# Scatters that add, and 13 of 16 feature groups held at once, in a segment-attention kernel

## Chip, cores and metric

The kernel runs on one core of one Trainium2 chip. The metric is the device time of one execution in microseconds (us), the median of several executions. Two sorts of chips took part. On those of the first sort the kernel before took 408 to 411 us (the first comparison and two of the four calls of experiments); on the quicker sort, 367 us (the other two calls). So times of different calls are not compared; ratios within a call, and lengths of stages within a trace, are. In the views of the profile PE is TensorE's matmuls, PEld its loads of weights, DVE VectorE, ACT ScalarE, POOL GpSimd and SPq the queue of SyncE; "issue" marks time in which an engine waited for nothing that the profile shows, "remote" a wait for something that it can't name.

## The reference

```python
# feat 16384 x 256 float32, bids: the segment (0..7) of each row, in no order
q, k, v = feat @ Wq, feat @ Wk, feat @ Wv          # dqk = 32
qp, kp, vp = pad(q), pad(k), pad(v)                # by segment, in order of rows, at most 3072
attn = softmax(where(mask, qp @ kp.T, NEG))        # pos = row number minus the first place of its segment
r = (attn @ vp)[bids, pos]
t = r @ Wt
tn = (t - t.mean(0)) / sqrt(t.var(0) + 1e-5) * gamma + beta
return feat + relu(tn)
```

The positions are computed as if the segments were sorted, and they are not, so most rows share one result. The kernel uses that: most rows of the output are `feat` plus one of a few rows `y`, and some 5,500 rows, the owners, have a result of their own.

## The kernel before

Attention goes segment by segment. GpSimd gathers the features of the owners into `xs` (48 tiles of 128 rows) and `xL` (3 tiles more, of rows found late). After the batch statistics the output stage has two parts. The dense part takes all 16384 rows as 16 groups of 1 MB: it loads a group, adds `hot.T @ y` to it and stores it. The owners' part normalises each owner's row, adds its features, and overwrites its row in the output by a scatter, after the dense store that it must follow. Overwriting needs the features of the owners in `xs` until the end.

```python
# attention, fifth segment: flags of edges, which the dense part needs as 0/1 matrices "hot"
for c in range(C):                                   # C = 8
    eb = hotp.tile([P, GT * P], BF16, tag="eb", bufs=2)
    nc.vector.memset(eb, 99.0)
    for r in range(2):
        nc.sync.dma_start(eb[64 * r : 64 * r + 3 * NE, :], edge_of[...].to_broadcast(...))
    nc.vector.tensor_scalar(hot[:, c, :, :], eb..., emod, None, ALU.is_equal)
# ... cut ...
# owners' rows, two tiles at a time: three VectorE passes, one of them with the features x
nc.vector.tensor_tensor(p, t, scale.to_broadcast([P, T, D]), ALU.mult)
nc.vector.tensor_tensor(p, p, shift.to_broadcast([P, T, D]), ALU.add)
nc.vector.scalar_tensor_tensor(t, p, 0.0, x, ALU.max, ALU.add)
# ... cut ...
for n, pair in enumerate(pairs):                     # 8 pairs of groups
    for k in pair:
        if k >= len(ahead):
            nc.sync.dma_start(f_bufs[k % IOB], feat3[ORDER[k]])     # IOB = 6 buffers
    for i in range(0, GT, 2):
        # ... TensorE: pf = hot.T @ y; in pairs 2 to 7 one of two groups also adds its features there ...
        # ... VectorE adds pf to the other group, ScalarE copies the first one back ...
        for _ in range(n_ops[n]):
            next(row, None)                          # a pass of the owners' rows
    for k in pair:
        dense.append(nc.scalar.dma_start(out3[ORDER[k]], f_bufs[k % IOB]).ins)
# ... cut ...
def put(y, at, after):                               # GpSimd, 48 + 3 times
    w = nc.gpsimd.indirect_dma_start(out=out, out_offset=..., in_=y, ...).ins
    for d in dense[after:]:
        tc.declare_no_dep(w, d)                      # waits for the first `after` stores only
```

Of the kernel before, what the change touches and what calls it, by code (L numbers as in the profile page):

```python
# [18 lines left out]
P = 128  # L19
# [16 lines left out]
IOB = 6  # L36
# [495 lines left out]
def segment_attention_bn_kernel(  # L532
# [44 lines left out]
    with ExitStack() as short:  # L577
# [49 lines left out]
        xL = fs.tile([P, LT, D], F32, name="xL")  # L627
# [35 lines left out]
        ]  # L663

# [207 lines left out]
        def list_tokens(e, h, pc):  # L872


            at = e * FT + 3 * h
            own3 = slice(at, at + 3)

            def col(c):
                return pc[:, :, c : c + 1].rearrange("p t x -> p (t x)")

            lr = fw.tile([P, 3], F32, tag="lr", name=f"lr_{e}")
            nc.vector.tensor_tensor(lr, rcol[:, 3 * h : 3 * h + 3], col(J), ALU.subtract)
            nc.vector.tensor_tensor(lr, lr, col(J + 1), ALU.subtract)
            jc = fw.tile([P, 3], F32, tag="jc", name=f"jc_{e}")
            for t in range(3):
                upto = fw.tile([P, J], F32, tag="upto", name=f"upto_{e}")
                nc.vector.tensor_scalar(
                    upto, pc[:, t, 0:J], lr[:, t : t + 1], None, ALU.is_le, ALU.add,
                    accum_out=jc[:, t : t + 1],
                )  # L890
            pad = fw.tile([P, 3], F32, tag="pad", name=f"pad_{e}")
            nc.vector.tensor_scalar(
                pad, valid[:, own3], 1.0, -float(N), ALU.subtract, ALU.mult
            )
            nc.vector.tensor_add(jc, jc, pad)
            nc.vector.tensor_tensor(idx[:, own3], jc, col(J + 2), ALU.add)
            for t in range(3):
                x = xs[:, at + t, :] if e < NB else xL[:, 3 * h + t, :]
                gather(x, feat, idx[:, at + t : at + t + 1], N)
# [164 lines left out]
        def attend(b, T):  # L1064
# [15 lines left out]
            if b == NB - 1:  # L1080
                nc.vector.tensor_add(E[:, 0, :], E[:, 0, :], e_late)
                nc.vector.tensor_mul(E[:, 1, :], E[:, 0, :], E[:, 0, :])
                for g, f in zip(ORDER, f_bufs):
                    nc.sync.dma_start(f, feat3[g])
                statistics()
# [280 lines left out]
        for a in range(NB // PART):  # L1366
# [4 lines left out]
            for arm in tc.Switch(tiles[a], 3**PART, hint=f"part{a}"):  # L1371

                T = [TMIN + arm // 3**i % 3 for i in range(PART)] + [FT]
                for i in range(PART):
# [11 lines left out]
                    if b + 1 < NB:  # L1386
                        first_scores(b + 1)
                    if b == 0:
                        positions()
                        load_reads(0)  # L1390
                        for x in (acc, E, xL, L, xs[:, (NB - 1) * FT :, :]):
                            zero(x.rearrange("p t d -> p (t d)"))
# [50 lines left out]
        def rows():  # L1443


            work = [(tk[:, ts(u, 2), :], xs[:, ts(u, 2), :]) for u in range(TT // 2)]
            for at in range(0, LT, 2):
                t = slice(at, min(at + 2, LT))
                work.append((L[:, t, :], xL[:, t, :]))
            for t, x in work:  # L1450
# [6 lines left out]
                yield  # L1457
                nc.vector.scalar_tensor_tensor(t, p, 0.0, x, ALU.max, ALU.add)  # L1458
# [9 lines left out]
        n_ops = [0, 0, 4, 4, 3, 3, 3, 3]  # L1468
        with tc.manual_schedule(engines={mybir.EngineType.DVE, mybir.EngineType.PE}):
            for n, pair in enumerate(pairs):  # L1470
                for k in pair:
                    if k >= len(ahead):
                        nc.sync.dma_start(f_bufs[k % IOB], feat3[ORDER[k]])
                for i in range(0, GT, 2):
# [3 lines left out]
                    for u in range(2):  # L1478
                        for k in pair:
                            half, c = ORDER[k] % 2, ORDER[k] // 2  # L1480
                            r = slice(64 * half, 64 * half + 3 * NE)
                            on_pe = n > 1 and k % 2
# [9 lines left out]
                    for k in pair:  # L1492
                        two = f_bufs[k % IOB][:, i : i + 2, :]
                        if n > 1 and k % 2:
# [5 lines left out]
                for k in pair:  # L1500
                    dense.append(nc.scalar.dma_start(out3[ORDER[k]], f_bufs[k % IOB]).ins)
                if n == 1:
# [12 lines left out]
        def put(y, at, after):  # L1515
# [6 lines left out]
                oob_is_err=False,  # L1522
            ).ins
# [61 lines left out]
```

## Time and profile before

| kernel before | value |
|---|---|
| runs ahead of the prediction | 409.6 us median of 3 (406.14 to 420.6) |
| the profiled execution | 397.4 us, span 395.6 us |
| statistics ready (first matmul that uses `y`) | 275.4 us |
| last matmul, after the statistics | +99.9 us |
| last scatter ends, after the statistics | +103.8 us |
| output stage: busy PE / DVE / ACT | 80.1 / 76.0 / 13.4 us of 99.9 |

The lines of the page and of the trace are shown in the prediction below. One reading of this table matters later: the profiled execution was 9 to 23 us quicker than the three timed ones.

### The profile page before, as it was taken

The page shows a single profiled execution, that of the slowest core. Times are in us where ns is not written, and L with a number is a line of the kernel's source. Part 1 is how long each engine was busy: PE and PEld are TensorE (multiplying, and loading weights), DVE is VectorE, ACT ScalarE, POOL GpSimd, SP SyncE. Part 2 cuts the span into 40 slices and gives each one's busy share as a digit, 9 for nine tenths or more (in the row PEclk, how much of TensorE's full clock was granted, in tenths as well). Part 3 has the DMA queues.
Part 4 walks back from the last instruction along what each step waited for, and adds up shares of the span by engine and source line. Part 5 has one row for each costly group of instructions (what it writes and reads, how often), then busy time and mean ns, then how long its engine had stood idle before and what let it go on. Part 6 is the DMA issues. An engine that isn't in the chain of part 4 may idle for free.

```text
span 395.6 us, 4145 instructions
## 1 busy us (share of the span) xinstructions
PE 288.5 (73%) x1139; PEld 178.3 (45%) x1139; DVE 262.8 (66%) x776; ACT 109.4 (28%) x208; POOL 170.2 (43%) x181
## 2 busy tenths in 40 slices
PE   1659596905889999389989499992897699099900
PEld 0436474603557578157855386661233243033300
DVE  8974699573778646488982166577999784198600
ACT  8424533202423541234233214530021110021100
POOL 3425166787540320377877400010314377454720
PEclk9978699977899999869999989996555555555555
DMA  5101012021121211211331010469799999745460
GB/s 109 35 14 56 5 56 86 11 74 50 43 59 58 65 35 55 60 44 40 100 107 49 0 51 30 160 231 368 284 398 370 397 400 381 275 178 235 177 240 4
DMA packets 20905, 53.34 MB, mean 135 GB/s; under 512 B 6606, under 2 KB 13344, under 8 KB 16746
## 3 DMA queue, kind: packets, MB, share of 16 engines
q1 hardware_dynamic: 11493, 25.06, 18.4%
q10 hardware_dynamic: 2421, 16.83, 10.4%
q0 software_dynamic: 6928, 10.81, 9.0%
q14 instruction: 48, 0.39, 0.4%
q8 instruction: 15, 0.25, 0.3%
HBM read 26.67 MB, written 29.92 MB: 143 GB/s over the span
## 4 chain that ended last, share of the span: by engine, by line
PE 46%; DVE 24%; issue 12%; another core or an unknown queue 5%; DMA 3%; ACT 3%; POOL 2%; DVEq 0%; POOLq 0%; ACTq 0%
PE po L1008 18%; PE pf L1488 8%; PE pv L953 7%; PE s L967 4%; DVE work L1497 3%; DMA work<-in_r_feat 3%; PE pf L1483 3%; PE px L922 2%; PE pqk L934 2%; POOL out L1516 2%; DVE tk L1013 2%; DVE py L1456 1%; DVE work L941 1%; DVE py L1454 1%
## 5 line engine op out<-in xcount | busy, mean ns | idle before, releaser
L1008 PE MATMUL po<-work 128*128 128x257 f32 x394 | 101.4, 405 | 14.0 <-issue 6.7
L1008 PEld LDWEIGHTS po<-work 128*128 128x128 f32 x394 | 77.4, 203 | 31.4 <-issue 10.3
L836 POOL DMA_INDIRECT xs<-in_r_feat,idx x48 | 50.9, 1061 | 64.8 <-issue 40.0
L1516 POOL DMA_INDIRECT out<-tk,idx x48 | 47.3, 984 | 45.0 <-DVE tk L1458 16.6
L836 POOL DMA_INDIRECT reads_r<-reads_of,idx x48 | 54.2, 1130 | 19.4 <-issue 15.1
L953 PE MATMUL pv<-wvt,work 128*128 128x256 f32 x164 | 39.4, 391 | 13.0 <-issue 11.6
L1483 PE MATMUL pf<-y,hot 48*128 48x256 bf16 x128 | 27.3, 391 | 20.4 <-ACT f L1495 9.5
L1488 PE MATMUL pf<-work,ident 128*128 128x256 f32 x64 | 39.0, 714 | 2.5 <-DMA work<-in_r_feat 2.5
L1497 DVE TENSOR_TENSOR work<-work,pf 128x512 f32<-128x512 f32 x40 | 26.1, 683 | 21.8 <-remote 14.4
L953 PEld LDWEIGHTS pv<-wvt,work 128*128 128x128 f32 x164 | 30.9, 193 | 21.3 <-issue 13.5
L972 ACT ACTIVATE work<-s,mask 128x512 f32<-128x512 f32 (+2 forms) x62 | 32.6, 601 | 17.7 <-PE s L967 12.4
L1012 DVE RECIPROCAL rdens<-po 128x1 f32<-128x1 f32 x39 | 6.1, 161 | 45.7 <-PE po L1008 21.4
L997 ACT ACTIVATE sq<-tk 128x256 f32<-128x256 f32 x39 | 16.3, 418 | 55.0 <-DVE tk L1013 47.4
L1483 PEld LDWEIGHTS <-hot 48*128 48x128 bf16 x128 | 7.1, 104 | 44.6 <-issue 44.5
L967 PE MATMUL s<-work 32*128 32x512 f32 (+2 forms) x124 | 24.8, 595 | 3.0 <-ACT work L972 3.0
L957 ACT COPY work<-pv 128x512 f32<-128x512 f32 (+1 forms) x21 | 12.1, 577 | 43.1 <-PE pv L953 25.3
L1495 ACT COPY work<-pf 128x512 f32<-128x512 f32 x16 | 9.4, 586 | 48.8 <-PE pf L1488 39.9
L922 PE MATMUL px<-ident,xs 128*128 128x128 f32 x82 | 15.8, 296 | 8.9 <-issue 2.9
L1488 PEld LDWEIGHTS pf<-work,ident 128*128 128x128 f32 x64 | 16.0, 310 | 11.8 <-issue 9.1
L934 PE MATMUL pqk<-work,wqk 128*128 128x512 f32 (+2 forms) x52 | 20.9, 539 | 0.2 <-issue 0.2
L998 DVE SCALAR_TENSOR_TENSOR acc<-sq,reads_r,acc 128x256 f32<-128x256 f32 x39 | 18.7, 481 | 1.2 <-ACT sq L997 0.7
L1488 PE MATMUL pf<-f,ident 128*128 128x256 f32 x32 | 19.5, 714 | 0.0
(241 smaller groups left out, 371.2 us busy)
## 6 DMA issues: line engine op xcount, KB each, us to landing
work<-in_r_feat SPq DMA_DIRECT2D x14, 1024.0 KB
out<-work ACTq DMA_DIRECT2D x14, 1024.0 KB
t_rows<-tk SPq DMA_DIRECT2D x3, 768.0 KB
t_rows<-tk SPq DMA_DIRECT2D x4, 512.0 KB
f<-in_r_feat SPq DMA_DIRECT2D x2, 1024.0 KB
out<-f ACTq DMA_DIRECT2D x2, 1024.0 KB
eb<-edge_of SPq DMA_DIRECT2D x16, 96.0 KB
t_rows<-tk SPq DMA_DIRECT2D x4, 256.0 KB
```

The lines of the kernel that those rows point to most:

```text
L836: nc.gpsimd.indirect_dma_start(out=dst, out_offset=None, in_=table, in_offset=bass.IndirectOffsetOnAxis(ap=ind, axis=0), bounds_check=n - ...
L922: nc.tensor.transpose(px[:, ts(t, P)], xs[:, b * FT + t0 + t, ts(h, P)], ident)
L934: nc.tensor.matmul(pqk[:, 0:w], wqk[:, h, :], xT[:, h, own_c], start=(h == 0), stop=(h == DH - 1),)
L953: nc.tensor.matmul(pv[:, t, :], xT[:, h, ts(t0 + t, P)], wvt[:, h, :], start=(h == 0), stop=(h == DH - 1),)
L967: nc.tensor.matmul(s[:, i, 0:w], k[g, t // 4, :], q[g, c : c + w], start=True, stop=True)
L972: nc.scalar.activation((pr_b if c else pr_a)[:, t, 0:w], s[:, i, 0:w], AF.Exp, bias=mask[:, m : m + 1],)
L998: nc.vector.scalar_tensor_tensor(acc[:, 1, :], sq, reads_r[:, one], acc[:, 1, :], ALU.mult, ALU.add)
L1008: nc.tensor.matmul(po, pr[:, t, ts(r, P)], v[:, t, :], start=(t == 0), stop=(t == T - 1))
L1483: nc.tensor.matmul(pfs[k][:, u, :], hot[r, c, i + u, :], y3[r, :], start=True, stop=not on_pe,)
L1488: nc.tensor.matmul(pfs[k][:, u, :], ident, f_bufs[k % IOB][:, i + u, :], start=False, stop=True,)
L1497: nc.vector.tensor_add(two, two, pfs[k])
L1516: w = nc.gpsimd.indirect_dma_start(out=out, out_offset=bass.IndirectOffsetOnAxis(ap=idx[:, at : at + 1], axis=0), in_=y, in_offset=None, b ...
```

## The change

The intent was to free the space of the owners' features. If the scatter adds to the output instead of overwriting it, the features are already there, put down by the dense store. `xs` is then dead after the projection, and six groups can be loaded onto it while attention still runs. One VectorE pass of the owners' rows goes away, and their ReLU moves to ScalarE. ScalarE gets more to do, so its stores go to SyncE.

```diff
-IOB = 6
+IOB = 13
-        xL = fs.tile([P, LT, D], F32, name="xL")
+        x_bufs = [xs[:, ts(g, GT), :] for g in range(TT // GT)]
+        f_bufs = x_bufs + f_bufs
@@ the loop over segments
                     attend(b, T[i])
                     if b + 1 < NB:
                         first_scores(b + 1)
+                    if b >= PART:                                  # PART = 4
+                        done = (b + 2) * FT
+                        for k in range(len(x_bufs)):
+                            if (done - FT if b > PART else 0) < (k + 1) * GT <= done:
+                                nc.sync.dma_start(x_bufs[k], feat3[ORDER[k]])
@@ owners' rows
-                nc.vector.scalar_tensor_tensor(t, p, 0.0, x, ALU.max, ALU.add)
+                nc.scalar.activation(t, p, AF.Relu)
@@ output stage
-        n_ops = [0, 0, 4, 4, 3, 3, 3, 3]
+        n_ops = [0, 2, 2, 2, 2, 2, 2, 2]
-                            on_pe = n > 1 and k % 2
+                            on_pe = n > 0 and k % 2
-                    dense.append(nc.scalar.dma_start(out3[ORDER[k]], f_bufs[k % IOB]).ins)
+                    dense.append(nc.sync.dma_start(out3[ORDER[k]], f_bufs[k % IOB]).ins)
+                    if k - 3 + IOB in range(IOB, NG):
+                        nc.sync.dma_start(f_bufs[k - 3], feat3[ORDER[k - 3 + IOB]])
@@ put
                 oob_is_err=False,
+                compute_op=ALU.add,
```

(Cut: the gathers and the zeroing of `xL`, the five loads onto `work`, and some reordering, among it that ScalarE's instructions of the output stage are put in a fixed order too.)

More of the change, by code (lines that the diff above doesn't have):

```diff
@@ L897, in list_tokens @@
             for t in range(3):
-                x = xs[:, at + t, :] if e < NB else xL[:, 3 * h + t, :]
-                gather(x, feat, idx[:, at + t : at + t + 1], N)
+                if e < NB:
+                    gather(xs[:, at + t, :], feat, idx[:, at + t : at + t + 1], N)
         def load_list(e):
@@ L1082, in attend @@
                 nc.vector.tensor_mul(E[:, 1, :], E[:, 0, :], E[:, 0, :])
-                for g, f in zip(ORDER, f_bufs):
-                    nc.sync.dma_start(f, feat3[g])
+                for k in range(len(x_bufs), len(f_bufs)):
+                    nc.sync.dma_start(f_bufs[k], feat3[ORDER[k]])
                 statistics()
@@ L1390, in segment_attention_bn_kernel @@
                         load_reads(0)
-                        for x in (acc, E, xL, L, xs[:, (NB - 1) * FT :, :]):
+                        for x in (acc, E, L, xs[:, (NB - 1) * FT :, :]):
                             zero(x.rearrange("p t d -> p (t d)"))
@@ L1443, in rows @@
         def rows():
-            work = [(tk[:, ts(u, 2), :], xs[:, ts(u, 2), :]) for u in range(TT // 2)]
-            for at in range(0, LT, 2):
-                t = slice(at, min(at + 2, LT))
-                work.append((L[:, t, :], xL[:, t, :]))
-            for t, x in work:
+            work = [tk[:, ts(u, 2), :] for u in range(TT // 2)]
+            work += [L[:, at : min(at + 2, LT), :] for at in range(0, LT, 2)]
+            for t in work:
                 T = t.shape[1]
@@ L1456, in rows @@
                 nc.vector.tensor_tensor(p, p, shift.to_broadcast([P, T, D]), ALU.add)
-                yield
-                nc.vector.scalar_tensor_tensor(t, p, 0.0, x, ALU.max, ALU.add)
+                nc.scalar.activation(t, p, AF.Relu)
                 yield
@@ L1467, in segment_attention_bn_kernel @@
         pairs = [(k, k + 1) for k in range(0, NG, 2)]
-        n_ops = [0, 0, 4, 4, 3, 3, 3, 3]
-        with tc.manual_schedule(engines={mybir.EngineType.DVE, mybir.EngineType.PE}):
+        n_ops = [0, 2, 2, 2, 2, 2, 2, 2]
+        for k in range(len(ahead), IOB):
+            nc.sync.dma_start(f_bufs[k], feat3[ORDER[k]])
+        with tc.manual_schedule(engines=set(ENGINES[:3])):
             for n, pair in enumerate(pairs):
-                for k in pair:
-                    if k >= len(ahead):
-                        nc.sync.dma_start(f_bufs[k % IOB], feat3[ORDER[k]])
                 for i in range(0, GT, 2):
@@ L1493, in segment_attention_bn_kernel @@
                         two = f_bufs[k % IOB][:, i : i + 2, :]
-                        if n > 1 and k % 2:
+                        if n > 0 and k % 2:
                             nc.scalar.copy(two, pfs[k])
@@ L1500, in segment_attention_bn_kernel @@
                 for k in pair:
-                    dense.append(nc.scalar.dma_start(out3[ORDER[k]], f_bufs[k % IOB]).ins)
-                if n == 1:
+                    dense.append(nc.sync.dma_start(out3[ORDER[k]], f_bufs[k % IOB]).ins)
+                    if k - 3 + IOB in range(IOB, NG):
+                        nc.sync.dma_start(f_bufs[k - 3], feat3[ORDER[k - 3 + IOB]])
+                if n == 0:
                     nc.vector.tensor_copy(scale[:, 0, :], scale_s)
```

## The prediction

> **What bounds the kernel now.** I read the page's picture of the span in 40 slices first, since the change touches one stage only, then the table of stretches, then the timeline of the last stage. A slice is 9.9 us.
>
> ```profile
> PE   1659596905889999389989499992897699099900
> DVE  8974699573778646488982166577999784198600
> PEclk9978699977899999869999989996555555555555
> DMA  5101012021121211211331010469799999745460
> ```
>
> The reader is to see three ages. Up to slice 26 (about 266 us) there is attention, with TensorE near full in most slices, near full clock, and little DMA. Then come the batch statistics, with TensorE idle. From 275 us on there is the output stage: clock 0.5, DMA at 9 for five slices and then at 4 to 7. In slices 34 and 35 PE falls to 0 and DVE to 1: something stops both.
>
> The table of stretches (engine busy us, then clock, DMA share, GB/s) cuts the last stage up:
>
> ```profile
> core 0: us, PE busy (x) PEld busy (x) DVE busy (x) ACT busy (x) POOL busy (x), PEclk, DMA share, GB/s
> ...
> 285.80:298.80 13.00, 10.51 (x31) 4.29 (x29) 12.66 (x22) 2.35 (x4) 2.10 (x3) 0.50 1.00 393
> ...
> 314.00:336.00 22.00, 21.27 (x58) 9.07 (x59) 13.11 (x21) 2.39 (x5) 16.82 (x18) 0.50 1.01 389
> 336.00:345.00 9.00, 0.37 (x1) 0.10 (x1) 0.00 (x0) 0.54 (x1) 5.09 (x6) 0.50 0.80 309
> ```
>
> From 286 to 336 the DMA engines are full at 390 GB/s; from 314 TensorE is full too; from 336 to 345 nothing computes. The timeline names the waits, and shows the step in which TensorE works and how the scatters are issued at the end:
>
> ```profile
> 298.75 1.22 PE L1488 MATMUL pf<-work,ident 128*128 128x256 f32 x2 [2.49 <-DMA work<-in_r_feat]
> ...
> 332.38 0.40 PE L1483 MATMUL pf<-y,hot 48*128 48x256 bf16 x2
> 332.71 0.50 PEld L1488 LDWEIGHTS pf<-f,ident 128*128 128x128 f32 x2 [0.22 <-issue]
> 332.71 1.22 PE L1488 MATMUL pf<-f,ident 128*128 128x256 f32 x2
> ...
> 345.06 0.69 DVE L1497 TENSOR_TENSOR work<-work,pf 128x512 f32<-128x512 f32 x1 [11.41 <-remote]
> ...
> 376.89 0.98 POOL L1516 DMA_INDIRECT out<-L,idx  x1 [0.30 <-issue]
> ...
> 378.18 0.99 POOL L1516 DMA_INDIRECT out<-L,idx  x1 [0.30 <-issue]
> ```
>
> So the output stage waits for feature groups: six buffers hold 16 groups, and a buffer is reloaded only after its store, behind a full DMA system. Between these waits TensorE sets the pace: the same 1.22 us piece begins every 1.48 us (332.71, 331.23, 329.75 in the timeline). The stage from 275.5 us to the last matmul at 375.3 us is 99.8 us: 9.6 us for the first two pairs, 48 steps (6 pairs of 8) x 1.48 = 71.0 us, and so 19 us of waits. The last scatter is issued at 378.2 us, the last stores at 377.7 to 378.5, and the span ends at 395.6: 17 us of landing and closing that no part of the change touches.
>
> **What the Trainium skill says.** "DMA: Bandwidth & Descriptors", section "SWDGE vs HWDGE vs iDMA", says that an accumulating DMA can be issued from GpSimd only; the scatters are already there, so no issue moves. It doesn't price an accumulate. "Collectives: The Full Stack", section "The bandwidth ceiling: the fold count and why AG ≠ RS ≠ AR", says that an add in flight reads two sources with two read descriptors, and so ran at half the rate of a copy. The trace of before has no accumulate, so it neither agrees nor differs. "DMA: Bandwidth & Descriptors", section "Issuing engines are not separate DMA queues", says that all issuers share the same 16 engines; the full DMA row with three queues active agrees. "TensorE: Matmul & The Clock Gate", section "Part 1: The HAM clock gate (the "warmup" mystery)", says that about 3.4 us of sustained work releases the full clock. The trace differs: from 314 to 336 us TensorE is 97% busy and its clock stays at 0.50. I go by the trace and keep 1.48 us a step.
>
> **The change part by part.**
> (a) Loads. Six groups go onto the space of `xs` after the fifth, sixth and seventh segments, five more onto `work` as before, two onto new tiles. So 13 of 16 are there or on the way as the stage begins, and the last three refill buffers whose stores finish two pairs into it. The 19 us of waits should vanish. The early loads (6 x 1.05 MB, 2.7 us each at 390 GB/s) fall between about 205 and 255 us, where the slices show under 110 GB/s and mostly far less.
> (b) VectorE. A pair of owners' tiles cost three passes of 0.69 us and now two; the third, a ReLU, goes to ScalarE. There are 24 whole items and 2 of `L`: 26 x 0.69 = 17.5 us leave VectorE. The adds of groups fall from 40 to 36, another 2.7. VectorE goes from the 76 us busy of 275.4 to 380 to about 56: per half-step 0.68 + 2 x 0.69 = 2.06 us against 2.96 us of TensorE. Not a bound.
> (c) TensorE. Pair 1 moves there as well, so 56 steps instead of 48: 56 x 1.48 = 82.9 us, 11.9 more, for one pair (about 4.8 us) less on VectorE. Stage: 4.8 + 82.9 = 87.7 us, from 275.5 to 363.2 instead of 375.3. Gain **12 us**: the waits of 19 us minus 7.
> (d) ScalarE. 28 copies instead of 24 and 26 ReLUs at about 0.59 us: 32 us, far from full. Its stores go to SyncE, which waits in order but carries few.
> (e) Scatters. The 51 are issued every 0.98 + 0.30 = 1.29 us. With an add, each of their some 5,500 rows of 1 KB also reads its old value: 5.6 to 6.5 MB more DMA reading, about the 6 MB of loads that leave the stage. The bytes of the stage stay near 33 to 35 MB, 85 to 90 us at 390 GB/s.
> When do they end? They wait for the first 3, 5, 7 or 11 stores, and for their rows, now one item per 2.96 us from 280: the last rows of the last segment at 351, of `L` at 357. Segments one to four need store 5, landed near 309, and then 24 scatters; in order, at 1.29 us, the last of 51 leaves at about 367, instead of 378.2. Gain **11 us**. I choose 10 as the sum of (c) and (e), which run side by side, less a microsecond for contention: span about 385.5, or 2.5% off.
> The clock of runs is not the profile: unprofiled runs gave 406 to 421, the profiled one 397. 409.6 x 0.975 is 399; I shade it to 398, since the stage suffers from full DMA and probably suffers more in the longer runs.
>
> **Rivals.**
> 1. The adding scatter becomes the bound. If three descriptors in place of two make its issue 1.9 us instead of 1.29, the last 45 after 309 us take 86 us and end at 395: slower than before by 17, near 425. At 1.6 us they end at 381 and nothing is gained. For it: two reads per row. Against it: gathers and scatters of different row sizes (4 bytes, 1 KB) all take 0.98 to 1.13 us here, so issue hardly depends on what is moved. Chance about 2 in 10 of losing most of the gain here.
> 2. The waits move into attention. Early loads share the DMA engines with gathers of indices' rows, and all engines but GpSimd stand still between 222 and 226 us for the last of such gathers. If 4 MB delay it, or block SyncE's row stores, 2 to 10 us come back. Against it: gathers have their own queue, and the DMA share there is 0.02. I count 1 us as likely: about 400.
> 3. The loads were hidden anyway and TensorE at half clock absorbs everything: pair 1 costs 12 us more on it. If only the 9 us standstill goes, gain is about 2, near 407.
> 4. TensorE, no longer starved, gets its full clock. Then DMA (88 us from 281, so 369) bounds, and no more than the 10 us come out. So the upside is short, except where the longer unprofiled runs gain more.
>
> **Range and chances.** 398 us as the middle; rivals 2 and 3 fill 400 to 412, a gain of 6% fills the other side: 384 to 412. Faster by over 2% means under 401.4: 0.57. Within 2%: 0.33. Slower needs rival 1 in full: 0.10.
>
> **What would show it.** In the trace of after: no waits for in_r_feat in the output stage and no standstill; TensorE steps still of 1.48 us and the last matmul near 363; scatters still about 1.29 us apart with the last near 367; ReLUs on ScalarE near 0.6 us; y ready near 275 as before. Scatters further apart than 1.5 us, statistics later than 278, or a clock other than 0.5 in the stage would each prove the sum wrong.

## The result

The changed kernel is correct and took **436.04 us** (434.32 to 436.54, 4 runs); the kernel before took 407.89 us (406.14 to 420.6, 4 runs). The ratio is **1.070**, 95% interval 1.064 to 1.077: slower. Ratios here and below are the mean time of one kernel's fast runs over the mean of the other's fast runs of the same rounds, so they are not quite the ratio of the medians.

The page's picture of the changed kernel, 40 slices of 10.8 us:

```profile
PE   1777696521999998475688999995699999994000
DVE  8972898206799737432369436467976756661000
POOL 3415247773050500377500550000107788888880
PEclk9989699955899999588689589999555555555555
DMA  4101012100222102481014301377999989999530
```

In the output stage PE is 9 from slice 29 to 35, without the fall to 0 that the picture of before has in slice 34 (the prediction says 34 and 35, but 35 is a 9 again): the standstill is gone, and TensorE waits for no load, as predicted. But a new row is full: POOL is at 8 for the last seven slices with work, two of them wholly after TensorE has ended. In attention PE has four weak slices in a row (16 to 19) at clocks of 0.5 to 0.8; the kernel before has one there (16).

The two groups of scatters, before and after (busy us, mean ns of one, then idle time ahead of them), and the new ReLU of two tiles:

```profile
L1516 POOL DMA_INDIRECT out<-tk,idx x48 | 47.3, 984 | 45.0 <-DVE tk L1458 16.6 <-issue 12.3 <-DVE py L1456 8.8
```

```profile
L1522 POOL DMA_INDIRECT out<-tk,idx x48 | 74.9, 1561 | 27.0 <-issue 11.9 <-ACT xs L1499 11.4 <-ACT tk L1463 2.2
...
L1463 ACT ACTIVATE tk<-py 128x512 f32<-128x512 f32 x24 | 14.3, 597 | 8.8 <-DVE py L1462 8.2 <-issue 0.6
```

A scatter that adds takes 1.56 us of GpSimd and not 0.98. With the 0.30 us between two, they begin every 1.86 us and not 1.29. The ReLU has the 0.6 us that was expected of it. The end of the timeline shows GpSimd alone, with no wait but "issue":

```profile
415.75 1.56 POOL L1522 DMA_INDIRECT out<-tk,idx  x1 [0.30 <-issue]
417.61 1.56 POOL L1522 DMA_INDIRECT out<-L,idx  x1 [0.30 <-issue]
419.48 1.56 POOL L1522 DMA_INDIRECT out<-L,idx  x1 [0.30 <-issue]
421.34 1.56 POOL L1522 DMA_INDIRECT out<-L,idx  x1 [0.30 <-issue]
```

The software queue, which carries gathers and scatters, before and after:

```profile
q0 software_dynamic: 6928, 10.81, 9.0%
```

```profile
q0 software_dynamic: 11680, 10.61, 13.5%
```

The bytes stay and the packets grow. The add alone makes it 4,896 packets, in the kernel before (11,824 in e3_before_add, below) as in the changed one (6,784 in e1_plain, without the add): 96 for each of the 51 scatters. More packets fit what the prediction cited of the Trainium skill, "Collectives: The Full Stack", section "The bandwidth ceiling: the fold count and why AG ≠ RS ≠ AR": an add reads two sources with two descriptors. But a second reading of bytes doesn't show: the queue's 10.81 MB and the page's HBM reads (26.67 MB) are the same in before and in e3_before_add, so the 5.6 to 6.5 MB more that the prediction counted are not seen in these counters.

Read by stage, in the two profiled executions:

| stage | before | after | difference |
|---|---|---|---|
| statistics ready | 275.4 | 306.6 | +31.2 |
| from there to the last matmul | 99.9 | 88.9 | -11.0 |
| from the statistics to the end of the last scatter | 103.8 | 116.3 | +12.5 |
| from the last scatter to the end of the span | 16.4 | 10.9 | -5.5 |
| span | 395.6 | 433.8 | +38.2 |

(First, third and fourth rows sum to the last.) TensorE did what was predicted, 88.9 us against 87.7, but it no longer sets the end. There are two losses, one at the scatters and one in attention, where only a microsecond had been allowed for. And 38 us is more than the 28 us between the medians: the profile of before is a lucky execution, which the experiments confirm.

### The profile page after: what moved, and what is told of

Read it like the earlier page. It is cut to its first block, busy times and chain, and to the rows that moved or that the text cites. A ratio compares the mean times of both kernels' runs of the same rounds, so it can differ in the third digit from the quotient of the medians.

```text
span 433.8 us, 4206 instructions
## 1 busy us (share of the span) xinstructions
PE 310.2 (72%) x1155; PEld 188.0 (43%) x1155; DVE 245.3 (57%) x746; ACT 126.2 (29%) x237; POOL 188.4 (43%) x178
## 5 line engine op out<-in xcount | busy, mean ns | idle before, releaser
L1522 POOL DMA_INDIRECT out<-tk,idx x48 | 74.9, 1561 | 27.0 <-issue 11.9
L955 PE MATMUL pv<-wvt,work 128*128 128x256 f32 x164 | 46.5, 439 | 32.6 <-ACT work L959 20.5
L838 POOL DMA_INDIRECT reads_r<-reads_of,idx x48 | 48.5, 1009 | 24.2 <-issue 19.6
L1492 PE MATMUL pf<-xs,ident 128*128 128x256 f32 x64 | 39.1, 714 | 0.0
L936 PE MATMUL pqk<-work,wqk 128*128 128x512 f32 (+2 forms) x52 | 27.4, 674 | 1.9 <-issue 1.9
L943 DVE COPY work<-pqk 32x128 f32<-32x128 f32 x41 | 11.9, 290 | 24.8 <-remote 9.7
L924 PEld LDWEIGHTS px<-ident,xs 128*128 128x128 f32 x82 | 10.5, 157 | 22.1 <-issue 10.5
L1501 DVE TENSOR_TENSOR xs<-xs,pf 128x512 f32<-128x512 f32 x20 | 13.1, 683 | 11.9 <-PE pf L1487 11.9
L1492 PE MATMUL pf<-work,ident 128*128 128x256 f32 x32 | 19.5, 715 | 0.0
L1492 PEld LDWEIGHTS pf<-xs,ident 128*128 128x128 f32 x64 | 16.0, 310 | 7.7 <-issue 7.7
```

The costliest lines, as they stand in the source:

```text
L838: nc.gpsimd.indirect_dma_start(out=dst, out_offset=None, in_=table, in_offset=bass.IndirectOffsetOnAxis(ap=ind, axis=0), bounds_check=n - ...
L924: nc.tensor.transpose(px[:, ts(t, P)], xs[:, b * FT + t0 + t, ts(h, P)], ident)
L936: nc.tensor.matmul(pqk[:, 0:w], wqk[:, h, :], xT[:, h, own_c], start=(h == 0), stop=(h == DH - 1),)
L955: nc.tensor.matmul(pv[:, t, :], xT[:, h, ts(t0 + t, P)], wvt[:, h, :], start=(h == 0), stop=(h == DH - 1),)
L1492: nc.tensor.matmul(pfs[k][:, u, :], ident, f_bufs[k % IOB][:, i + u, :], start=False, stop=True,)
L1501: nc.vector.tensor_add(two, two, pfs[k])
```

## The experiments

Each theory is about one of the two losses. **Scatter theory:** GpSimd's issue of 51 adding scatters at 1.86 us sets the end. Its rival: the DMA engines, with more to read, hold the end up. **Queue theory:** SyncE issues in order, and early loads that wait for their space stand ahead of the flags of edges, for which VectorE waits in order, for which TensorE waits. Its rivals: the bytes of the early loads, or the changed order of everything else (instructions in attention are ordered automatically, and a small edit reorders a part of them), or chance.

### e1_plain: the change without the add

```diff
-                compute_op=ALU.add,
```

The owners' rows lose their features, so the result is wrong on purpose (relative error 0.44); the work is otherwise the same.

> The changed kernel, but its scatters overwrite instead of adding (owners' rows come out wrong on purpose: the features are missing in them). Order of all instructions is the same. Theory: the add itself makes each scatter's issue 1.86 us from one to the next instead of 1.29, so here the 45 scatters that run without a pause return to 1.29 and the last leaves about 26 us earlier after y is ready (90 us after it instead of 116); then the stores, at 363-365 us on the old clock, end the stage, so the total falls by 20 to 26 us, to about 412. Attention stays as long as in the changed kernel (y ready near 306 in the profile). Rival: the issue is slowed by full DMA rings behind 2 MB pair stores; then the pitch stays at 1.8 and the total within 5 us of 436.

Measured: 420.15 us (418.71 to 421.42), ratio to before 1.030 (1.023 to 1.037). Statistics at 304.0 us, scatters 1.29 us apart, last scatter 96.4 us after the statistics. Against the changed kernel's profile the span is 416.8 instead of 433.8, with statistics only 2.6 us apart: the add costs some 14 to 17 us, and the loss in attention is there without it. By the medians the time fell by 16 us, less than the 20 to 26 expected, since the last matmul came at +96.6 and not at +89: a stand is back in which VectorE waits 3.6 us for "remote" (see e13_next_plain).

### e3_before_add: the kernel before with the add alone

```diff
-                nc.vector.scalar_tensor_tensor(t, p, 0.0, x, ALU.max, ALU.add)
+                nc.vector.tensor_scalar(t, p, 0.0, None, ALU.max)
+                compute_op=ALU.add,
```

> The kernel before, with one part of the change alone: scatters add, and the third pass of the owners' rows leaves the features out (still on VectorE, one operand less). The order of instructions is unchanged, the result stays right. Theory (issue of an add costs 0.57 us more): scatters 1.86 us apart; the 24 that run in a row take 45 us instead of 31 and the whole chain of 51 ends some 15 to 25 us later, so 420 to 432 against 408. Rival (adds cost nothing of their own): within 3 us of before. y ready at the same time as in before, to 2 us in the profile, but for the spread that before itself shows.

Measured: correct, 420.82 us (419.59 to 421.76), ratio 1.031 (1.025 to 1.038). The last matmul came at 375.1 us and the last scatter ended at 406.4, so scatters bound this kernel too, with early loads nowhere. (The last matmul is at +89.4 here, with six buffers; the changed kernel with 13 has +88.9.) The two groups of this profile and of e1_plain's:

```profile
L1516 POOL DMA_INDIRECT out<-tk,idx x48 | 74.9, 1561 | 32.2 <-DVE work L1497 11.9 <-issue 11.3 <-DVE py L1456 7.2
```

```profile
L1522 POOL DMA_INDIRECT out<-tk,idx x48 | 47.3, 985 | 36.8 <-ACT tk L1463 19.5 <-issue 12.5 <-ACT work L1499 4.2
```

The add alone makes 0.985 into 1.561 us, in either kernel, to within a nanosecond. In the changed kernel it is 1.56 us too where the DMA share is 1.01 (336 to 345 us) and where it is 0.59 (396 to 423 us). So the time is that of the issue and not a wait for full DMA engines; the scatter theory holds. This run has a second use. Its order of instructions is that of before up to the output stage, and its statistics came at 285.7 us, not 275.4. In the first profile of before the second segment's rows were stored at 96.5 us, here at 110.9. ScalarE had stood 13.3 us for "remote" in that segment there, and stands 26.0 us here: that execution was some 10 us ahead of what this order gives on such a chip, and the prediction started from it.

### e2_late: early loads where the other five are

```diff
-                    if b >= PART:
-                        done = (b + 2) * FT
-                        ... four lines: load x_bufs after the fifth to seventh segment ...
-                for k in range(len(x_bufs), len(f_bufs)):
+                for k in range(len(f_bufs)):
```

> The changed kernel, but the six early loads onto the space of the features are issued after attention, together with the five onto the work space. Theory: part of the 31 us that attention lost comes from those loads standing at the head of SyncE's queue (waiting for the transposes) before the 16 loads of edge flags, and from 4 MB beside the gathers: y is ready 10 to 20 us earlier than in the changed kernel. The rest is the new automatic order, which stays different from before here too. Output stage: 11 loads of 1 MB need about 29 us, so its first pairs wait up to 20 us, unless they are issued early enough. Rival (early loads cost nothing, only the order does): y ready within 4 us of the changed kernel's 306.

Measured: correct, 419.31 us (417.12 to 427.42, one run of the four slow), ratio of fast runs 1.025 (1.016 to 1.034). Statistics at 289.2 instead of 306.6, everything after them as in the changed kernel (+89.0, +116.6). The automatic order pulled the loads forward again: SyncE issued them from 178.9 us on. So this isn't a run without early loads. It is one in which they stand between the flags and not in front of them. That is worth 17 us, and it speaks for the queue theory and against the bytes. It doesn't decide alone, since the order of other instructions changes with it.

### e2_xl_early: the gathers of `xL` kept

The code for `xL` is put back into the changed kernel (with 12 buffers), to see whether its removal is what reorders attention.

> The changed kernel with the zeroing and the three gathers of the second feature copy put back (their result is not used), and 12 instead of 13 groups held, for space. The early loads stay. Theory: the change removed one ScalarE operation and three gathers, and with that the automatic order of the first four segments changed; with them back that part is ordered as before, so the fourth segment ends some 10 us earlier (near 163 us instead of 175), while the part behind the early loads stays slow: y ready near 295. Rival (the early loads alone do it): y ready near 306 as in the changed kernel; second rival (order alone): near 277.

Measured: correct, 431.61 us median, in two clusters (422.81 and 424.9; 438.31 and 439.61). Statistics at 294.9 in the profiled, fast run. The fourth segment ended at 170.3 us, as in the changed kernel (170.9), so the detail that was expected of it missed. Inconclusive: another order, another loss.

### e5_thin: an eighth of the bytes asked for at the same place

```diff
-                                nc.sync.dma_start(x_bufs[k], feat3[ORDER[k]])
+                                nc.sync.dma_start(x_bufs[k][:, 0:1, :], feat3[ORDER[k]][:, 0:1, :])
```

(The other seven tiles of each group come with the five late loads.)

> The changed kernel; of each of the six early groups only one of eight tiles (128 KB instead of 1 MB) is loaded at the early place, the other seven with the loads onto the work space (though the automatic order may move those forward, as it did in the run with the loads issued late, where they came out between the loads of edge flags). Result right. Theory (what costs is the place at the head of SyncE's queue, before the edge flags, and the order that comes of it, not the bytes): y stays ready later than 298 in the profile if the six thin loads still stand before the flags. Rival (4 MB of traffic beside the gathers costs it): y ready at 286 to 291, total near 420.

Measured, on a quicker chip (before 367.45 us there): correct, 403.64 us (401.23 to 404.74), ratio **1.096** (1.089 to 1.104). Statistics came at 274.9 us; on chips of this sort before has them at 255.9 and the change at 263.7 (before_again and after_again, below). So it is slower than the change itself. But it is no test of the bytes: the automatic order pulled the other seven tiles forward too (`xs` on L1086 in the lines below, among the flags). What its profile shows, more plainly than any other, is how a load can hold up the flags. SyncE's timeline (start, length, what), the queue's own waits, and the waits of the engines between 180 and 205 us:

```profile
160.91 2.07 SPq L1220 DMA_DIRECT2D eb<-edge_of  x4
163.28 0.35 SPq L1086 DMA_DIRECT2D xs<-in_r_feat  x1
168.17 18.66 SPq L1397 DMA_DIRECT2D xs<-in_r_feat  x2
187.06 0.33 SPq L1086 DMA_DIRECT2D xs<-in_r_feat  x1
187.49 1.76 SPq L1220 DMA_DIRECT2D eb<-edge_of  x4
```

```profile
SPq L1397 <- DMA xs<-in_r_feat,idx: 17.9, 1, 17.9
```

```profile
DVE hot L1226 <- DMA eb<-edge_of: 15.9, 2, 15.3
...
PE po L1010 <- DVE tk L1015: 15.3, 1, 15.3
```

A small load waits 17.9 us for a gather into its space. The flags stand behind it from 163 to 187. VectorE waits 15.3 us for the flags, TensorE 15.3 us for VectorE's next normalisation. What costs here is where a load of 128 KB stands in the queue and what it waits for. It is not the same stand as in the change: the edit moved the loads, and the one that waits here is one of the later two.

### e7_hybrid: adds for half of the segments

A half of the scatters overwrite as before (segments 4 to 7, whose features stay in `xs`), 27 add, 10 buffers, loads placed as in e2_late.

> A version meant to beat both: only the rows of segments 0 to 3 and of the list L are added by scatters (27 of 51), segments 4 to 7 keep their features and are overwritten as before; three groups go onto the space of segments 0 to 3, five onto work, two onto new tiles; loads issued late. Result right. Sum: 18 adds at 1.86 us and 24 + 3 others behind the start at 32.5 us after y: 32.5 + 18 x 1.86 + 24 x 1.29 + 3 x 1.86 = 103 us after y for the last scatter instead of 116, TensorE ends 89 after y; span y + 114. With y at 286 to 290: 400 to 404, total 402 to 406 against 409 of before: faster by 1 to 2%. If early loads or order still cost attention (y at 295 or later), no gain.

Measured: correct, 377.66 us (375.17 to 379.02), ratio 1.025 (1.018 to 1.033). Fewer adds lose less (last scatter +106.5 us after the statistics), but the kernel, meant to be 1 to 2% faster, still doesn't beat the one before.

### e9_before_noreads and e9_after_noreads: both kernels without the gathers of indices

```diff
-                gather(reads_r[:, m : m + 1], reads_of, idx[:, m : m + 1], N)
+                pass
```

Wrong on purpose (relative errors of about 1.3). The question was whether the loss in attention is a collision of early loads with gathers.

> The kernel before without the 48 gathers of 4 bytes that fetch how often a row is read (the statistics come out wrong on purpose). In both kernels TensorE's completions arrive late, one in 1.4 to 4 us, in stretches in which GpSimd issues such gathers without a pause (81 to 106 us, 190 to 217 us). Theory: these stretches vanish; y ready 20 to 30 us earlier than the typical 286, near 260. Rival (these stretches have nothing to do with the gathers): y ready within 8 us of 286.

> The changed kernel without the same 48 gathers (wrong on purpose). Theory: what the early loads cost attention (20 us against the typical run of before) comes out of the meeting of their place in the queue with such a stretch (190 to 217 us); without the gathers y is ready within 8 us of the other kernel without them. Rival (the early loads cost by themselves, by their traffic or by the edge flags behind them): the difference of the two stays 15 to 20 us.

Measured: 358.13 us (356.12 to 359.8) and 389.37 us (388.7 to 391.06), ratios 0.975 and 1.060 to the kernel before. Between the two, statistics differ by 7.3 us (250.1 and 257.4), the last scatter after them by 20.8 (+96.4 and +117.2). The loss in attention remains without these gathers (on this sort of chip it is 7.8 us with them), so a collision with them isn't needed for it. The bounds of the expectations were set for the first sort of chip: 7.3 us lies within the 8 us of the collision theory, but here that tells nothing. The statistics of the kernel before came only 5.8 us earlier than with the gathers (255.9), where 20 to 30 were expected.

### before_again and after_again: both kernels on the same, quicker chip

> The kernel before, unchanged, for a second profile. If the first profile was an unusually good one, statistics come at 280 to 287 us on a chip of the first speed (about 257 on the quicker chip), not at 275.4, and the time is that of the other runs of before. If it was typical, 275.4 comes again. Scatter pitch 1.29 us either way. The standstill at the end of the output stage is either there again (9 us) or, as in the run of before without gathers of reads, not.

> The kernel after, unchanged, on the same chip as the others of this call. Theory of two terms: scatters 1.86 us apart, last scatter some 116 us after the statistics; statistics 15 to 20 us later than in the kernel before of this call on a chip of the first speed. Rival (the attention loss was a chance of one execution): statistics within 5 us of before, ratio near 1.03.

Measured: before 368.67 us in the profiled run (the seven others 365.51 to 368.32); after 392.39 us (391.33 to 393.9), ratio **1.069** (1.064 to 1.074), as on the first chip. Here the two profiles are of ordinary executions:

| stage, quicker chip | before_again | after_again | e10_next (below) |
|---|---|---|---|
| statistics ready | 255.9 | 263.7 | 257.8 |
| to the last matmul | +90.3 | +89.1 | +89.0 |
| to the end of the last scatter | +96.8 | +115.7 | +116.2 |
| last scatter to the end of the span | 14.1 | 10.9 | 10.9 |
| span | 366.8 | 390.3 | 384.9 |

So 23.5 us are 7.8 in attention plus 18.9 at the scatters minus 3.2 at the close. The last matmul of before stands at +90.3, not at +99.9: TensorE's two longest waits in the stage are 4.0 us (for a load) and 3.8 us (for VectorE) here, and the standstill of 9.5 us isn't there at all. The expectation of 15 to 20 us in attention was for the other sort of chip.

### e10_next: four early loads, one segment later

```diff
-                    if b >= PART:
+                    if b > PART:
-                            if (done - FT if b > PART else 0) < (k + 1) * GT <= done:
+                            if (done - FT if b > PART + 1 else 0) < (k + 1) * GT <= done:
```

> After, with the four early loads of the first stretch of xs asked for one segment later (with the sixth segment's, not the fifth's), so that none of them stands in SyncE's queue ahead of the flags of edges. Queue theory: the flags are no longer held behind loads that wait for TensorE's reads of xs; statistics 10 to 18 us earlier than in after of this call, TensorE's idle stretches around the fifth segment gone; output stage unchanged (last matmul +89, last scatter +116 after the statistics); ratio to before 1.02 to 1.035. Rival (the loads cost by their bytes or by the changed order of the rest): statistics as late as in after, ratio as after's.

Measured: correct, 385.27 us (384.1 to 386.81), ratio 1.048 (1.044 to 1.052) against 1.069 for the change in the same call. Statistics 5.9 us earlier than in the change and 1.9 us later than in before; the output stage is unchanged. The gain is smaller than the 10 to 18 us expected, because there were only 7.8 to be had on this chip, and the ratio lies outside the 1.02 to 1.035 expected. SyncE's queue in after_again and then in e10_next:

```profile
156.73 9.82 SPq L1395 DMA_DIRECT2D xs<-in_r_feat  x4
166.77 19.84 SPq L1218 DMA_DIRECT2D eb<-edge_of  x12
```

```profile
157.68 0.36 SPq L1395 DMA_DIRECT2D xs<-in_r_feat  x1
159.99 1.74 SPq L1218 DMA_DIRECT2D eb<-edge_of  x4
```

In the change four loads wait for TensorE to have turned what lay in their space (7.4 us for one of them), and the first flag is asked for at 166.8 us. In e10_next one load is ahead of it, and the flags begin at 160.0; the automatic order put the other three between the flags, as in e2_late. Now what the delay does. TensorE's timeline in after_again:

```profile
191.34 0.52 PE L869 MATMUL pc<-lcx,oh 128*128 128x131 bf16 x6
194.28 2.81 PE L1010 MATMUL po<-work 128*128 128x257 f32 x8 [2.41 <-DVE hot L1224]
```

TensorE stood for 2.41 us because VectorE was busy with a late flag matrix (`hot`). That is little. The table of stretches of 4 us shows what followed, first for after_again, then for e10_next (the column after the busy times is the granted clock):

```profile
core 0: us, PE busy (x) PEld busy (x) DVE busy (x) ACT busy (x) POOL busy (x), PEclk, DMA share, GB/s
...
191.00:195.00 4.00, 1.59 (x13) 1.02 (x10) 3.91 (x9) 2.19 (x5) 3.39 (x3) 1.00 0.42 140
195.00:199.00 4.00, 4.00 (x10) 1.63 (x9) 4.00 (x22) 0.95 (x2) 2.44 (x2) 0.54 0.02 2
199.00:203.00 4.00, 4.00 (x14) 2.29 (x12) 1.18 (x6) 0.74 (x2) 2.88 (x3) 0.50 0.20 60
203.00:207.00 4.00, 4.00 (x6) 1.51 (x5) 0.00 (x0) 1.99 (x4) 3.09 (x4) 0.50 0.86 297
```

```profile
191.00:195.00 4.00, 2.89 (x21) 1.54 (x20) 3.90 (x16) 1.97 (x5) 3.09 (x4) 1.00 0.22 73
195.00:199.00 4.00, 4.00 (x16) 1.90 (x15) 1.89 (x13) 1.16 (x3) 3.09 (x4) 1.00 0.03 2
199.00:203.00 4.00, 4.00 (x16) 2.41 (x15) 1.37 (x5) 0.37 (x1) 3.09 (x4) 1.00 0.64 184
203.00:207.00 4.00, 4.00 (x19) 2.72 (x18) 0.90 (x2) 3.27 (x7) 3.08 (x4) 1.00 0.51 198
```

With the stand, the clock falls to 0.5 from 195 to about 208 us while TensorE is busy all the time; without it, the clock stays at 1.00. At half clock TensorE begins 30 matmuls in these 12 us instead of 51. The kernel before keeps 1.00 in these stretches too. The stores of rows give the price: from the fifth segment's last store to the sixth's first one takes 23.9 us in before_again and in e10_next, and 30.0 us in after_again. The pair without gathers shows the same: 23.9 us in e9_before_noreads, 30.0 us in e9_after_noreads, where TensorE is busy for 1.88 of 4 us and then has a clock of 0.50 for 12 us. So most of the loss in attention on this chip (6.1 of 7.8 us) is half a clock for 13 us, after a short stand; that the queue brought the stand about follows from the late flags and from e10_next, but the edit there also changes the order of other instructions.

### e12_flags_act: flags from ScalarE's queue

```diff
-                    nc.sync.dma_start(
+                    nc.scalar.dma_start(
                         eb[64 * r : 64 * r + 3 * NE, :], ...
```

> After, with the flags of edges loaded from ScalarE's queue and not SyncE's; early loads stay where they are. Queue theory: flags no longer wait behind the early loads, statistics 8 to 18 us earlier than in after of this call, unless ScalarE itself stands while it waits for the cleared buffers (then a loss of a few us on ScalarE that shows as its idle time). Rival: statistics as late as in after. Output stage the same in both: last scatter +116 us after the statistics.

Measured: correct, 392.57 us (391.11 to 393.62), ratio 1.070, as slow as the change; statistics at 261.9. The sixth segment's stretch is back at 23.9 us and its clock with it. But the fifth segment, between the last stores of the fourth and of the fifth, takes 51.0 us instead of 45.1 (44.2 in before_again). ScalarE issues in order too, so flags that wait for a cleared buffer now can hold the exponentials and copies behind them. This may be the loss on ScalarE that was named beforehand as the possible exception, but it is argued from these lengths, not shown by a wait; the one wait for flags that the trace has is VectorE's, of 4.5 us, so the flags came late from this queue too.

### e13_next_plain: all of the change but the two causes

This is e10_next without `compute_op=ALU.add` (a wrong result on purpose, relative error 0.44).

> The kernel with its four early loads asked for one segment later, and with overwriting scatters (a wrong result on purpose): all of the change but the add and but the place of those loads in SyncE's queue. Theory of two terms: nothing of the loss is left; scatter pitch 1.29 us, statistics within 3 us of before, last scatter some 96 us after the statistics, ratio to before between 0.99 and 1.01. Rival (more loads, SyncE's stores or pair 1 on TensorE cost by themselves): ratio over 1.015 with scatters at 1.29 us.

Measured, on a chip of the first sort: 403.17 us (402.72 to 403.82). The kernel before took 410.81 us (400.44 to 418.57) there; a single quick run of it set the bar for its state, all others were counted as slow, and no ratio is given. Without the two causes nothing of the loss is left: the ratio of the medians is 0.98 (expected 0.99 to 1.01), and that to the single quick run 1.007. The rest, predicted to be worth 10 us, is worth 7.6 us by the medians, within the spread of the kernel before. The fifth segment took 43.8 us; it had taken 64.7 in the changed kernel, 64.5 in e1_plain, and 43.7 in e3_before_add, all on chips of this sort. So moving the four loads gives 21 us back there. By what path is not shown: in the changed kernel's trace no engine waits for the flags to land, and TensorE's only wait for a flag matrix is 2.1 us.

The profile has another lesson. With 13 groups held, and no load to wait for, there is again a standstill late in the output stage (first the stretch of 7 us, then VectorE's wait):

```profile
346.00:353.00 7.00, 0.22 (x2) 0.00 (x0) 0.94 (x2) 0.33 (x2) 2.78 (x3) 0.50 0.19 65
```

```profile
DVE work L1501 <- remote: 8.6, 1, 8.6
```

All engines but GpSimd stand nearly all the time, DMA is at 0.19, and VectorE waits for "remote". The standstill of 9.5 us in before (337 to 346) was of this kind too (its `work` addition had waited 11.41 us for "remote"), and was not, or not all, a wait for groups. It appears on the first sort of chip, in stretches in which GpSimd issues every 1.29 us without a pause. All five profiles of the first sort with plain scatters have waits for "remote" in the output stage (the longest 3.6 to 11.8 us), the four with adding ones (after, e3_before_add, e2_late, e2_xl_early) have none, and on the quicker chips no profile has one anywhere. The same sort of stand is in attention on chips of the first sort, where GpSimd gathers without a pause; TensorE and ScalarE stand there, VectorE a part of the time. In e3_before_add:

```profile
105.46 1.07 ACT L957 COPY work<-pv 128x512 f32<-128x512 f32 x2 [26.01 <-remote]
```

On the quicker chip the second segment was done at about 85 us instead of 110. What makes these stands is open.

### e4_before_sp: the kernel before, stores by SyncE

```diff
-                    dense.append(nc.scalar.dma_start(out3[ORDER[k]], f_bufs[k % IOB]).ins)
+                    dense.append(nc.sync.dma_start(out3[ORDER[k]], f_bufs[k % IOB]).ins)
```

> The kernel before with its group stores issued by SyncE and not ScalarE, alone. Neutral theory: ratio within 0.99 to 1.01. Rival (SyncE waits in order, so a store not yet ready holds the next load): the stage grows by some 4 us or more, ratio over 1.01.

Measured in the same call: correct, 418.3 us (417.28 to 422.41) against the median of 410.81 for before. The last matmul comes 109.0 us after the statistics (99.9 in the first profile of before). SyncE's timeline, and TensorE's longest wait in the stage:

```profile
312.10 0.33 SPq L1501 DMA_DIRECT2D out<-f  x1
312.49 0.42 SPq L1473 DMA_DIRECT2D work<-in_r_feat  x1
312.97 0.90 SPq L1501 DMA_DIRECT2D out<-work  x1
313.91 10.04 SPq L1473 DMA_DIRECT2D work<-in_r_feat  x4
```

```profile
PE pf L1488 <- DMA work<-in_r_feat: 13.6, 1, 13.6
```

Loads wait behind stores that wait for their group to be finished; TensorE stands 13.6 us for a load. With 6 buffers SyncE is the wrong issuer for the stores; the change escapes this only because 13 of its groups are there already. The direction is the rival's; by the spread of before it is not a verdict.

### e11_L_add: adds where they are nearly free

Before, with `xL` dropped: only the 3 scatters of `L` add, and the space holds a seventh buffer. (The expectation speaks of six gathers saved; there are three.)

> The kernel before with the second way used only where it is nearly free: the features of L's owners are not gathered, its 3 scatters add, its ReLU is on ScalarE, and the freed space holds one more group (7 buffers and not 6). Theory: 3 x 0.57 = 1.7 us for the adds at the end of the chain, six gathers of 1.1 us less in attention, and one wait for a group less; ratio 0.985 to 1.005, correct. Rival: the changed order in attention costs or gives more than that, shown by when the statistics come.

Measured: correct, 411.95 us (407.97 to 422.88, one run of five slow) against 410.81 for before: no difference to be seen. No version here beats the kernel before.

## Why the prediction was wrong

- **Step (e), the scatters, failed.** "The 51 are issued every 0.98 + 0.30 = 1.29 us" was carried over to scatters that add; they measure 1.56 + 0.30 = 1.86 us. Rival 1 had this case (1.9 us, measured 1.86) and priced it well: 86 us for the last 45 scatters, measured 45 x 1.86 = 84. It got a chance of 2 in 10, on the ground that gathers and scatters of different sizes take about the same issue time. That was evidence on the size of rows; the add changes the number of packets, by 96 for each scatter. Cost on the whole time: 11.6 us in the kernel before (e3_before_add, 420.8 minus 409.2), 14 to 17 us in the changed kernel (e1_plain against it), and 15.7 us on the quicker chip (18.9 of the scatters minus 3.2 at the close, there with all else that the change does to the stage).
- **Step (a), the loads, failed.** Rival 2 named SyncE ("block SyncE's row stores, 2 to 10 us") and was counted as 1 us. The argument was on bytes and DMA shares, and e2_late and e10_next, which load the same bytes in the same part of attention, give 17.4 and 5.9 us of it back. What waited behind the loads was not the row stores but the flags of edges, and the diff doesn't show them at all: they were found only by listing what the queue issued. Cost: 21 us in the fifth segment on the first sort of chip (the edit gives them back; the path through the flags is not seen in that trace), 7.8 us on the quicker one, 5.9 of which e10_next gives back. (A slip on the way: of the slices of the early loads, the one from 247 to 257 us shows 160 GB/s and not under 110.)
- **Step (c) was right in its own figure and wrong in its gain.** The stage to the last matmul is 88.9 us (predicted 87.7), no load is waited for, the clock is 0.50. But "the 19 us of waits" were read as waits for groups, and those of one execution were taken for the rule. TensorE's three longest waits after the statistics, in the first profile of before, are these:

```profile
PE pf L1483 <- ACT f L1495: 9.5, 1, 9.5
...
PE ps_bad L1440 <- DVE odd L1438: 3.8, 1, 3.8
...
PE pf L1488 <- DMA work<-in_r_feat: 2.5, 1, 2.5
```

  Only 2.5 us are put down to a load. The 3.8 us are VectorE's, and the 9.5 us are the standstill, behind a copy on ScalarE that had itself waited for "remote". In before_again the same sum gives 9.7 us of waits and the last matmul is at +90.3. With plain scatters on the first sort of chip the change has +96.6 (e1_plain) and +98.7 (e13_next_plain), since the standstill comes back with 13 groups held; and with adding scatters six groups do as well as 13 (+89.4 in e3_before_add). Of the 12 us of gain, 1 to 3 are left when like is compared with like; the smooth TensorE row of the changed kernel goes with its slow scatters, which end later.
- **The starting point was off.** Statistics "near 275" was an execution some 10 us quicker than that order gives on such a chip (e3_before_add: 285.7). The prediction saw the difference between 397 and 406 to 421 and scaled it, where it should have asked which stage differs.
- **Steps (b) and (d) held:** VectorE 59 us busy in the stage (predicted about 56), ReLUs at 0.597 us, ScalarE 31 us (predicted 32). A slip in (b): 26 x 0.69 is 17.9, not 17.5.

Open: what "remote" stands for in the standstills of the first sort of chip; why the misplaced loads cost 21 us there and 8 on the quicker chip (the second part is shown to be the clock there; on the first sort of chip the same stretch, 30.1 us, is as long with well-placed loads); and whether moving loads acts by the queue alone, since each such edit also changes the automatic order of other instructions. That an add costs 0.57 us at the issue is shown in both kernels, in the changed one with nothing else altered; why it takes GpSimd longer is not shown.

## What to carry to other kernels

Before a plain operation is replaced by a variant of it (here a scatter by an adding one), measure one of the variant; a mean duration of its relatives is not evidence, and on an engine that issues 51 in a row 0.57 us each becomes the bound. A load issued early on an in-order queue can cost by what it waits for and by what stands behind it, so list that queue in both orders before counting its bytes. And compare the profiled run with the timed ones: if it is quicker, its waits and stage times are not the typical ones.

## What the Trainium skill lacked or had wrong

- "DMA: Bandwidth & Descriptors", section "SWDGE vs HWDGE vs iDMA", says that an add in flight must be issued by GpSimd, but not what it costs there: 1.56 us of GpSimd for each adding scatter of 128 rows against 0.98 us for a plain one, the same in both kernels and on both sorts of chips.
- "Collectives: The Full Stack", section "The bandwidth ceiling: the fold count and why AG ≠ RS ≠ AR", says that adds read two sources with two descriptors. The packets fit (6,928 to 11,824 by the add alone), the counted bytes don't rise. That an add costs first in the issuing engine's time, and not in DMA bandwidth, no page says; the DMA share was 0.59 while the last scatters ran.
- "TensorE: Matmul & The Clock Gate", section "Part 1: The HAM clock gate (the "warmup" mystery)", says that about 3.4 us of sustained work gives the full clock and a whole idle window of that length takes it. Here the clock stayed at 0.50 through the output stage with TensorE busy 86.6 of 89 us. In attention it fell after a stretch of 4 us in which TensorE was busy for 1.59 us (longest idle 2.41 us), stayed low for about 13 us of full work, and did not fall where it was busy for 2.89 of 4; in e9_after_noreads it fell likewise after 1.88 of 4.
- No page has the standstills of TensorE and ScalarE (and for most of them VectorE) in stretches in which GpSimd issues without a pause: ScalarE's waits for "remote" are up to 26.0 us on one sort of chip, and on the other no engine has such a wait.
